# Zeros' term beside the last third of the quantized product, and the next pair's bias pass behind the first convolution's differences

## The chip, the cores and the metric

The kernel runs on one core of a Trainium2 chip. The metric is the device time of one execution in microseconds. The engines that matter here are TensorE (PE in the profile), VectorE (DVE), ScalarE (ACT), GpSimd (POOL), and SyncE (SP), which only issues transfers here. Each engine works through its own queue in order. Engines wait for one another by semaphores.

## What is computed

The input x holds 32 samples of 64 channels by 1024. Two layers follow one another, each with a conditioned chain of four small convolutions (same, upsample with blur, same, blur with downsample) and a product behind it, added to x:

```
x = x + L0_ffn(L0_cond(x, cond))     # gated low-rank experts
x = x + L1_ffn(L1_cond(x, cond))     # product with an int4 weight
# L1_ffn:
W[i, o] = scales[o] * q[i, o] - zeros[o]        # q: 4-bit whole numbers
out = einsum('bsi,io->bso', t, W) + bias
```

For the last line this means that an output is `scales * (t @ q) - zeros * rowsum(t) + bias`, and the residual x is added. `zeros * rowsum(t)` is the zeros' term of the title.

## The kernel before, in words

Two samples share the 128 partitions, so there are 16 pairs per layer. The change lies in the last stage, the second layer's loop over `k` from 16 to 31 (line 1290). In round k the product of pair p = k - 16 runs (`layer1`), and woven into it are the later half of the convolutions of the next pair (`later`, that is `rest`, once for each half h of the pair), the first convolution of the pair after that (`conv`, that is `first`, also once for each half) and the composition of its weights (`weights` and `compose`). `layer1` is a generator: it yields between pieces, and the loop at line 1296 puts the other work between the yields.

**The product.** The 1024 columns plus two (one column of ones, so that column 0 of the product is the row sum) are cut into three thirds c = 0, 1, 2 of 342 columns. For each third PE adds up sixteen matmuls into a PSUM bank (line 1039), eight with the high part of the input tokens and eight with the low part. Then:
- at c = 0, line 1054 takes the negated row sum `nrs` from column 0, and line 1055, one DVE operation over 128x1024, adds `zeros * nrs` to the whole output tile `o`;
- at every c, line 1057 (DVE) multiplies the bank by the scales into `s`, and line 1058 (POOL) adds `s` to its third of `o`;
- after c = 2, line 1060 (SP) sends `o` out.

**The bias pass.** `with_bias(p + 1)` (line 1018; its operation is line 1022, POOL, 128x1024) makes the next pair's `o` from its residual `xb` and the bias. `load_x1` (line 1015, SP) brings `xb`. Both tiles, and all `o` tiles, rotate through three buffers of one tag, so a bias pass can begin only when an older `o` has been sent out.

**The convolutions.** `first` makes `yt` on ACT (line 661), two DVE operations from PSUM (line 666), two DVE differences of SBUF operands (line 671), and then two POOL differences of these (line 674). `rest` is a chain on DVE: 717, 723, 746, the predicated copy 747 (it overwrites the outer columns of a PSUM bank with `re` where a mask from `ident` says so), 148, 773. Line 148 also releases ACT's line 774, behind which on ACT's queue stand the weight copies of lines 594 to 597 and the next `yt` of line 661. `composed2` has the POOL sums of lines 599 and 605.

**What sets the order.** The kernel text is an order of emission. A scheduler in the language builds each engine's queue from it when the program is built: it takes an operation that is ready in its own reckoning, the earlier emitted first. So an operation can stand in a queue far from its line. `tc.issue_after(v)` says that what is emitted in its block stands behind `v` on v's engine: an order of issue only, not a wait.

In round p the pieces are emitted in this order: third 0, high; third 0, low with its end; `later` h = 0; third 1, high; `conv` h = 0; third 1, low with its end; `later` h = 1; third 2, high; `weights`; third 2, low with `with_bias(p + 1)` and its end; `conv` h = 1; `compose`; the sending out.

Of the kernel before, what the change touches and what calls it, by code (L numbers as in the profile page):

```python
# [62 lines left out]
def adaln_ffn_kernel(ctx: ExitStack, tc: tile.TileContext, t, out: bass.AP):  # L63
    nc = tc.nc
# [13 lines left out]
    def cpst(name):  # L78
        return cps.tile([P, H], F32, tag="cps", name=name)
# [4 lines left out]
    def fpst(name):  # L84
        return fps.tile([P, H], F32, tag="fps", name=name)
# [35 lines left out]
    def xdv(n):  # L121
        return cv[:, (n % 2) * XD : (n % 2 + 1) * XD]

    def xev(n):

        o = O_XE + (n % 2) * XE
        return cv[:, o : o + XE]
# [25 lines left out]
    done, tbl, outers = {}, {}, {}  # L153
# [497 lines left out]
    def first(i, n, y):  # L651

        a = al0[:, n : n + 1]
        xe = xev(n)
        w = c0 if i == 0 else xdv(n)[:, : 3 * P].rearrange("p (a b) -> p a b", a=3)
        mid = cpst(f"c{i}_{n}_1")[:, :HQ]
        nc.tensor.matmul(mid, w[:, 1], xe[:, :HQ], start=True, stop=True)  # L659
        yt = wk.tile([P, HQ], F32, tag="yt", name=f"yt{i}_{n}", bufs=2)  # L660
        nc.scalar.activation(yt, mid, AF.Identity, bias=be0[:, n : n + 1], scale=a)  # L661
        yb, yo = y[:, :HQ], y[:, YO : YO + HQ + 1]
        for q, w_, d, o in ((0, HQ, yb, 2 * HQ - 1), (2, HQ - 1, yo[:, 1:HQ], HQ)):
            ps = cpst(f"c{i}_{n}_{q}")[:, :w_]
            done["c"] = nc.tensor.matmul(ps, w[:, q], xe[:, o : o + w_], start=True, stop=True)  # L665
            nc.vector.scalar_tensor_tensor(d, ps, a, yt[:, :w_], ALU.mult, ALU.add)  # L666
        nc.vector.memset(yb[:C, 0:1], 0.0)
        nc.vector.memset(yb[C:, HQ - 1 : HQ], 0.0)
        d = y[:, YD:YO].rearrange("p (a b) -> p a b", a=2)
        for k in range(2):  # L670
            nc.vector.tensor_tensor(d[:, k], yo[:, k : k + HQ], yb, ALU.subtract)  # L671
        e = y[:, YE:].rearrange("p (a two b) -> p a two b", a=2, two=2)
        for k in range(2):
            nc.gpsimd.tensor_tensor(  # L674
                e[:, :, k], d[:, :, 2 * k : 2 * k + HQ - 2 : 2], d[:, :, 1 : HQ - 1 : 2], ALU.subtract
            )
        return y
# [113 lines left out]
    def at(k):  # L791

        return k ^ 1
# [218 lines left out]
    def load_x1(p):  # L1012
        if p < NP:
            v = wk.tile([P, L], F32, tag="w4", name=f"xb_{p}", bufs=3)
            nc.sync.dma_start(v, x1d[p].rearrange("p f j -> p (f j)"))
            residual[NP + p] = v

    def with_bias(p, aux):

        if p < NP:  # L1020
            o = residual[p] = wk.tile([P, L], F32, tag="w4", name=f"o1_{p}", bufs=3)
            nc.gpsimd.tensor_tensor(
                o.rearrange("p (j f) -> p j f", f=4),
                residual.pop(NP + p).rearrange("p (f j) -> p j f", f=4),
                aux[:, 2].rearrange("p (j f) -> p j f", f=4),
                ALU.add,
            )

    def layer1(p, wq, aux):


        o = residual.pop(p)
        for c in range(3):
            if c == 1:
                load_x1(p + 1)
            ps = fpst(f"q{p}_{c}")[:, :QC]
            for j, half in enumerate(toks[f"x1_{p}"]):
                for k in range(NC):
                    nc.tensor.matmul(  # L1039
                        ps,  # L1040
                        half[:, k],
                        wq[at(k)][:, c * QC : (c + 1) * QC],
                        start=(k == 0 and j == 0),
                        stop=(k == NC - 1 and j == 1),
                    )
                if j == 0:
                    yield
            if c == 2:
                with_bias(p + 1, aux)
            a = 2 if c == 0 else 0  # L1050
            cs = slice(c * QC + a - 2, (c + 1) * QC - 2)
            if c == 0:
                nrs = tiny.tile([P, 1], F32, tag="nrs", name=f"nrs{p}")
                nc.vector.tensor_scalar_mul(nrs, ps[:, 0:1], -1.0)
                nc.vector.scalar_tensor_tensor(o, aux[:, 1], nrs, o, ALU.mult, ALU.add)  # L1055
            s = wk.tile([P, QC], F32, tag="yt", name=f"sc{p}_{c}", bufs=2)[:, : QC - a]
            nc.vector.tensor_tensor(s, ps[:, a:], aux[:, 0, cs], ALU.mult)  # L1057
            nc.gpsimd.tensor_tensor(o[:, cs], o[:, cs], s, ALU.add)  # L1058
            yield
        nc.sync.dma_start(out[p], o)  # L1060
# [35 lines left out]
    def conv(k, h, y=None):  # L1096
        if k < len(todo):
            i, n = todo[k][0], 2 * todo[k][1] + h
            y = yv(n) if y is None else y
            ys.setdefault(k, []).append(first(i, n, y))  # L1100
            if i == 1:
                load(k + 1, h)
# [187 lines left out]
    for k in range(NP, 2 * NP):  # L1290
        begin(k + 2)
        tables_of(k + 3)
        outer_of(k + 2)
        main = layer1(k - NP, *second)
        next(main)
        for fs in (
            (),
            ((later, k + 1, 0),),
            ((conv, k + 2, 0),),
            ((later, k + 1, 1),),  # L1300
            ((weights, k + 2),),
        ):
            for f, *v in fs:
                f(*v)
            if k == NP + 1:
                next(set_ends, None)
            next(main)
        conv(k + 2, 1)
        compose(k + 3)
        run(main)  # L1310
        if k == NP:
            set_ends = ends(1, LAST, NP, block(7, [P, 3 * AW], F32, "room3"))
        elif k == NP + 1:
            run(set_ends)
# [44 lines left out]
```

## Time and profile before

| what | value |
|---|---|
| three runs | 956.99, 960.23, 962.82 us (median 960.23) |
| profiled execution, its own time | 961.61 us |
| its span, first to last instruction | 959.8 us |
| granted TensorE clock, mean | 0.979 |
| PE, DVE, ACT, POOL busy | 888.5, 727.6, 324.0, 469.2 us |
| last stage: start of the bias pass in rounds 2 and 14 | 707.17 and 936.56 us |
| L747 (DVE, predicated copy), 24 of them from 707 to 937 us | 432 ns the shortest, mean 1055 ns |
| L1055 (DVE, zeros' term), 13 there | mean 1294 ns |
| L1022 (POOL, bias pass), 16 | 2862 / 2900 / 3882 ns, shortest / median / longest |
| L674 (POOL, differences), 50 from 700 to 940 us | median 616 ns |

A busy time is a sum over the whole span. The chain of work that ended last is followed back from the last instruction to whatever released each step. The timeline lists instructions in order of time, a start and a duration in microseconds, and in square brackets how long the engine sat idle before one and who released it. Two instructions merged in one line are marked x2, and their duration is that of both.

### The profile page before, as it was taken

How to read it: one execution, taken by the hardware profiler on the slowest of the kernel's cores; microseconds unless marked ns; L12 is line 12 of the kernel's file. 1: busy time of each engine (PE TensorE's matmuls, PEld its weight loads, DVE VectorE, ACT ScalarE, POOL GpSimd, SP SyncE). 2: the span in 40 equal slices, each digit the busy share in tenths (PEclk: the TensorE clock that was granted, in tenths of full speed). 3: DMA queues.
4: the chain of work that ended last, by engine and by line, in shares of the span. 5: the costliest groups of instructions: out<-in, count | busy, mean ns of one | idle time of the engine just before them, and what ended most of it. 6: DMA issues, size and time to landing. Idle time of an engine off the chain costs nothing.

```text
span 959.8 us, 14770 instructions
## 1 busy us (share of the span) xinstructions
PE 888.5 (93%) x5069; PEld 789.5 (82%) x5069; DVE 727.6 (76%) x1505; ACT 324.0 (34%) x702; POOL 469.2 (49%) x601
## 2 busy tenths in 40 slices
PE   5778879999999999999999999988899999999996
PEld 4656669999999999984778887778899899988986
DVE  6847786888887788658986666478888888888885
ACT  4224442444443333332431221263233323332320
POOL 4454463444545544455652222234756655665563
PEclk9888979999999999999999999999999999999999
DMA  5721121222222321344566765464322332333221
GB/s 126 232 56 50 50 61 59 74 83 83 72 72 81 85 93 67 111 173 139 169 193 203 208 200 181 154 210 143 105 89 91 114 121 89 102 102 121 83 83 45
DMA packets 48443, 109.81 MB, mean 114 GB/s; under 512 B 12580, under 2 KB 20896, under 8 KB 48368
## 3 DMA queue, kind: packets, MB, share of 16 engines
q1 hardware_dynamic: 46208, 103.42, 34.9%
q0 software_dynamic: 1200, 4.46, 1.4%
q10 hardware_dynamic: 960, 0.99, 0.4%
q8 instruction: 40, 0.66, 0.3%
q14 instruction: 35, 0.29, 0.1%
HBM read 70.97 MB, written 37.88 MB: 113 GB/s over the span
## 4 chain that ended last, share of the span: by engine, by line
PE 30%; DVE 14%; issue 4%; ACT 3%; POOL 2%; DMA 2%; ACTq 0%; POOLq 0%; SPq 0%; DVEq 0%
PE o L806 14%; PE q L1039 6%; PE f L579 2%; PE c L665 2%; DVE cv L671 2%; PE r L701 2%; DVE o L1055 1%; DVE cv L666 1%; PE r L732 1%; DVE r L747 1%; DVE rt L723 1%; DVE r L546 1%; DVE x L967 1%; PE ht L922 1%; PE r L709 1%
## 5 line engine op out<-in xcount | busy, mean ns | idle before, releaser
L674 POOL TENSOR_TENSOR cv<-cv 128x256 f32<-128x256 f32 x124 | 82.5, 665 | 127.3 <-DVE su L849 75.9
L774 ACT CAST thx<-h 128x512 fp32r<-128x512 f32 x60 | 37.1, 618 | 154.5 <-DVE h L148 154.4
L671 DVE TENSOR_TENSOR cv<-cv 128x257 f32<-128x257 f32 x124 | 87.2, 736 | 0.6
L666 DVE SCALAR_TENSOR_TENSOR cv<-c,al,yt 128x257 f32<-128x257 f32 x124 | 56.6, 476 | 31.2 <-ACT yt L661 29.8
L701 PE MATMUL r<-cv 128*128 128x128 f32 x496 | 70.6, 285 | 9.2 <-POOL cv L599 7.8
L1039 PE MATMUL q<-wq,thx 128*128 128x342 f32 x384 | 73.8, 334 | 5.6 <-ACT thx L774 5.6
L701 PEld LDWEIGHTS r<-cv 128*128 128x128 f32 x496 | 66.7, 198 | 12.3 <-POOL cv L599 8.4
L661 ACT ACTIVATE yt<-c,be,al 128x257 f32<-128x257 f32 x64 | 36.3, 568 | 110.9 <-PE c L659 104.5
L1039 PE MATMUL q<-wq,tlx 128*128 128x342 f32 x384 | 73.1, 333 | 0.0
L717 DVE TENSOR_TENSOR rt<-r,tbl 128x256 f32<-128x256 f32 x64 | 26.5, 415 | 61.3 <-PE r L709 57.9
L806 PE MATMUL h<-wa,tdx 128*128 128x352 f32 (+1 forms) x336 | 70.5, 348 | 0.0
L579 PE MATMUL f<-gs,iw 128*128 128x128 f32 (+1 forms) x384 | 70.0, 330 | 0.0
L599 POOL TENSOR_TENSOR cv<-cv 128x256 f32<-128x256 f32 x62 | 46.0, 743 | 47.3 <-ACT cv L597 47.3
L579 PEld LDWEIGHTS f<-gs,iw 128*128 128x128 f32 x384 | 63.4, 193 | 6.5 <-ACT room L519 0.3
L1039 PEld LDWEIGHTS q<-wq,thx 128*128 128x128 f32 x384 | 61.2, 191 | 7.6 <-ACT thx L774 7.0
L1058 POOL TENSOR_TENSOR o<-o,sc 128x342 f32<-128x342 f32 (+1 forms) x48 | 48.2, 1005 | 39.0 <-DVE sc L1057 31.4
L732 PE MATMUL r<-cv 128*128 128x128 f32 x496 | 65.8, 275 | 0.0
L806 PE MATMUL h<-wa,thx 128*128 128x352 f32 (+1 forms) x336 | 64.3, 333 | 0.0
L1039 PEld LDWEIGHTS q<-wq,tlx 128*128 128x128 f32 x384 | 62.8, 192 | 0.7
L806 PE MATMUL o<-wb,thh 128*128 128x512 f32 x224 | 61.7, 407 | 1.1 <-ACT wb L352 0.7
L806 PE MATMUL h<-wa,tlx 128*128 128x352 f32 (+1 forms) x336 | 62.4, 327 | 0.0
L786 POOL TENSOR_TENSOR tdx<-thx,tlx 128x1024 fp32r<-128x1024 f32 x14 | 36.1, 2580 | 52.9 <-ACT tlx L778 48.1
(302 smaller groups left out, 2150.3 us busy)
## 6 DMA issues: line engine op xcount, KB each, us to landing
cv<-in_x_dram SPq DMA_DIRECT2D x64, 256.0 KB
cv<-x1e SPq DMA_DIRECT2D x64, 192.5 KB
x1e<-dd SPq DMA_DIRECT2D x16, 514.0 KB
hgd<-hs SPq DMA_DIRECT2D x16, 512.0 KB
hg<-hgd SPq DMA_DIRECT2D x16, 512.0 KB
x1d<-x SPq DMA_DIRECT2D x16, 512.0 KB
xb<-x1d SPq DMA_DIRECT2D x16, 512.0 KB
out_dram<-o SPq DMA_DIRECT2D x16, 512.0 KB
```

What stands on the lines that cost most here:

```text
L579: done["f"] = nc.tensor.matmul(pv[:, n : n + 2 - k], iw[:, e].rearrange("p a b -> p (a b)"), v, start=(m == 0), stop=(m == len(steps) - 1) ...
L599: (nc.vector if once else nc.gpsimd).tensor_tensor(f[:, 4 * P : 6 * P].rearrange("p (a b) -> p a b", b=P), v[:, :, 0], v[:, :, 1], ALU.add,)
L661: nc.scalar.activation(yt, mid, AF.Identity, bias=be0[:, n : n + 1], scale=a)
L666: nc.vector.scalar_tensor_tensor(d, ps, a, yt[:, :w_], ALU.mult, ALU.add)
L671: nc.vector.tensor_tensor(d[:, k], yo[:, k : k + HQ], yb, ALU.subtract)
L674: nc.gpsimd.tensor_tensor(e[:, :, k], d[:, :, 2 * k : 2 * k + HQ - 2 : 2], d[:, :, 1 : HQ - 1 : 2], ALU.subtract)
L701: nc.tensor.matmul(ps[:, j * P : (j + 1) * P], y[:, j + k : j + k + 2 * P - 1 : 2], w(4 + k), start=(k == 0), stop=(k == 1),)
L732: done["r"] = nc.tensor.matmul(ps[:, j * P : (j + 1) * P], y[:, YE + (2 * q + k) * P : YE + (2 * q + k + 1) * P], w(q + 2 * k), start=True ...
L774: nc.scalar.copy(hi, h)
L806: nc.tensor.matmul(banks[l == 2], toks[key][l][:, order(k)], w[:, cols], start=(k == first and l != 1), stop=(k == last and l in (2, min(n ...
L1039: nc.tensor.matmul(ps, half[:, k], wq[at(k)][:, c * QC : (c + 1) * QC], start=(k == 0 and j == 0), stop=(k == NC - 1 and j == 1),)
L1058: nc.gpsimd.tensor_tensor(o[:, cs], o[:, cs], s, ALU.add)
```

## The change

Three edits:
- `first` keeps the second of its POOL differences (line 674) under the name `done["e"]`.
- `with_bias(p + 1)` is emitted after the high half of third 2, before the yield and so before `weights`, and it is tied behind `done["e"]`, the differences of `conv` h = 0 of the same round. Before, it was emitted after the low half of third 2 and tied to nothing.
- The zeros' term (line 1055) is emitted at c = 2, ahead of that third's scaling, instead of at c = 0. `nrs` is still made at c = 0.

```
@@ first
         for k in range(2):
-            nc.gpsimd.tensor_tensor(
+            done["e"] = nc.gpsimd.tensor_tensor(
                 e[:, :, k], d[:, :, 2 * k : 2 * k + HQ - 2 : 2], d[:, :, 1 : HQ - 1 : 2], ALU.subtract
             )
@@ layer1
                 if j == 0:
+                    if c == 2:
+                        with tc.issue_after(done["e"].ins):
+                            with_bias(p + 1, aux)
                     yield
-            if c == 2:
-                with_bias(p + 1, aux)
             a = 2 if c == 0 else 0
             cs = slice(c * QC + a - 2, (c + 1) * QC - 2)
             if c == 0:
                 nrs = tiny.tile([P, 1], F32, tag="nrs", name=f"nrs{p}")
                 nc.vector.tensor_scalar_mul(nrs, ps[:, 0:1], -1.0)
+            if c == 2:
                 nc.vector.scalar_tensor_tensor(o, aux[:, 1], nrs, o, ALU.mult, ALU.add)
```

More of the change, by code (lines that the diff above doesn't have):

```diff
@@ L673, in first @@
         for k in range(2):
-            nc.gpsimd.tensor_tensor(
+            done["e"] = nc.gpsimd.tensor_tensor(
                 e[:, :, k], d[:, :, 2 * k : 2 * k + HQ - 2 : 2], d[:, :, 1 : HQ - 1 : 2], ALU.subtract
@@ L1046, in layer1 @@
                 if j == 0:
+                    if c == 2:
+                        with tc.issue_after(done["e"].ins):
+                            with_bias(p + 1, aux)
                     yield
-            if c == 2:
-                with_bias(p + 1, aux)
             a = 2 if c == 0 else 0
@@ L1054, in layer1 @@
                 nc.vector.tensor_scalar_mul(nrs, ps[:, 0:1], -1.0)
+            if c == 2:
                 nc.vector.scalar_tensor_tensor(o, aux[:, 1], nrs, o, ALU.mult, ALU.add)
```

## The prediction

> **What bounds the kernel now.** I read first the page's busy times, then busy times by stretch for one round of the last stage, then the chain of waits through that round, then the DVE and POOL timelines of it. All edits lie in that stage.
>
> ```profile
> PE 888.5 (93%) x5069; PEld 789.5 (82%) x5069; DVE 727.6 (76%) x1505; ACT 324.0 (34%) x702; POOL 469.2 (49%) x601
> ```
>
> Over the span PE looks like the bound. The busy times of one round (from bias pass to bias pass: length, then PE, weight load, DVE, ACT, POOL) say something else:
>
> ```profile
> 802.95:821.99 19.04, 17.83 (x116) 16.92 (x116) 16.17 (x32) 6.13 (x14) 11.21 (x13) 1.00 0.33 104
> ```
>
> PE lacks 1.2 us of the round. The chain (start, length, what) shows who holds it:
>
> ```profile
> 816.13 0.58 ACT yt L661
> ...
> 816.73 0.88 DVE cv L666 x2
> ...
> 820.52 1.19 DVE o L1055
> 821.71 0.34 DVE rt L717
> ...
> 822.08 0.70 DVE rt L723
> ...
> 822.92 0.67 PE c L665 x2
> ```
>
> PE's L665 waits for DVE's L723 to free a PSUM bank, and L1055 stands in front of that. DVE and POOL in the same round:
>
> ```profile
> 803.84 0.70 DVE L746 TENSOR_TENSOR r<-r,rt 128x512 f32<-128x512 f32 x1
> 804.57 1.57 DVE L747 COPY_PREDICATED r<-ident,re 128x256 f32<-128x256 int32 x1
> ...
> 808.83 1.47 DVE L671 TENSOR_TENSOR cv<-cv 128x257 f32<-128x257 f32 x2
> 810.22 0.41 DVE L717 TENSOR_TENSOR rt<-r,tbl 128x256 f32<-128x256 f32 x1
> ...
> 811.47 0.70 DVE L746 TENSOR_TENSOR r<-r,rt 128x512 f32<-128x512 f32 x1
> 812.20 0.43 DVE L747 COPY_PREDICATED r<-ident,re 128x256 f32<-128x256 int32 x1
> 812.67 0.69 DVE L148 TENSOR_SCALAR h<-r 128x512 int32<-128x512 int32 x1
> ...
> 814.00 0.50 DVE L1057 TENSOR_TENSOR sc<-q,aux 128x342 f32<-128x342 f32 x1
> 816.73 0.88 DVE L666 SCALAR_TENSOR_TENSOR cv<-c,al,yt 128x257 f32<-128x257 f32 x2 [2.23 <-ACT yt L661]
> ```
> ```profile
> 802.95 2.90 POOL L1022 TENSOR_TENSOR o<-xb,aux 128x1024 f32<-128x1024 f32 x1 [1.41 <-DMA out_dram<-o]
> ...
> 810.45 1.31 POOL L674 TENSOR_TENSOR cv<-cv 128x256 f32<-128x256 f32 x2 [0.42 <-DVE cv L671]
> 815.07 0.74 POOL L599 TENSOR_TENSOR cv<-cv 128x256 f32<-128x256 f32 x1 [3.31 <-ACT cv L597]
> ```
>
> DVE is busy without a break but for 2.23 us. That gap starts when L148 of half 1 (ended 813.36) releases ACT's L774. Behind it stand the six weight copies and `yt`, 3.37 us until DVE's L666. So the round is: DVE from L666 to the end of L148 of half 1, plus 3.37 us of ACT. Whatever is added to or taken from DVE in between counts; what falls into the gap is free up to 2.23 us. Note L747: 0.43 us in half 1, 1.57 us in half 0, where it ends 0.29 us after the bias pass on POOL.
>
> **The change, part by part** (per round, rounds 2 to 13: twelve that have all pieces; X is the end of the second L671 of half 0, 810.30 in this round).
>
> *Zeros' term off third 0.* One L1055, 1.19 us of spacing on the chain: -1.19.
>
> *Bias pass off half 0.* The twelve L747 of half 0 last from 1.16 to 2.34 us, sum 20.1, mean 1.68, against 0.43 unhindered: -1.25. The wait for the sent-out tile (1.41 us idle on POOL) goes too, but it was off the chain.
>
> *Bias pass behind the differences.* L674's pair starts 0.15 after X and ends 1.46 after it. With nothing else in the way L1022 follows at X+1.42 and ends at X+4.32. On DVE L717, L723 and L746 follow X as before ([...]L746 took 0.70 beside L1022 too), and L747 of half 1 comes at X+1.90, half a microsecond after POOL has begun. It would end at X+4.61 instead of X+2.33: +2.28, straight into L148. [...] By the rows (0.43 against 1.57, end tied to POOL's) it is held[...]. I take the rows. [...]it swaps a collision of 1.25 us for one of 2.28.
>
> *Where the zeros' term lands.* It is emitted behind `later` of half 1, but a queue is filled by readiness. In the first layer's stage the trace shows what becomes of ready operations while the chain 717, 723, 746 waits for its own results:
>
> ```profile
> 254.70 0.41 DVE L717 TENSOR_TENSOR rt<-r,tbl 128x256 f32<-128x256 f32 x1
> 255.03 0.78 DVE L638 SCALAR_TENSOR_TENSOR cv<-cv,sty 128x257 f32<-128x257 f32 x1
> 255.75 0.67 DVE L723 TENSOR_TENSOR rt<-r,rt 128x512 f32<-128x512 f32 x1
> ```
>
> They are put between its links. In the last stage L666 of half 0 stands between L148 and L773, although emitted behind both; and L1022 ran in front of third 0's add, emitted at third 2. L1055's last input is POOL's add of third 1 (L1058, 808.99 for 1.03 us, so ended at X-0.28). It is thus ready about when L717 is, five links before L148, and I take it to stand there, either side of L717. In half 1 of before no other ready work competes for these places. The cost: L1055 from X-0.08 to X+1.19 [...]now holds POOL off:
>
> ```profile
> 684.81 3.88 POOL L1022 TENSOR_TENSOR o<-xb,aux 128x1024 f32<-128x1024 f32 x1
> ```
>
> (0.98 over its 2.90, beside an L1055 from 684.63 to 685.93). So the first L674 ends at X+1.67, the second at X+2.36, L1022 runs X+2.32 to X+5.22, and L747 (ready at X+3.09) ends at X+5.51 instead of X+2.33: +3.18, in place of the +2.28. Between L717 and L723 it comes to the same within 0.05. From below: were L1055 behind L148, it would fall into the 2.23 us gap and cost only what it delays POOL's L599 and the add of third 2, behind which the second L671 of half 1 then waits: 0 to 0.3. From above: behind L746 or L747 the whole 1.19 comes after the bias pass: +3.47.
>
> *The rest.* The new place of `load_x1` on SP: it waits for the bias pass's buffer and now comes some 8 us later in the round; behind it stand loads used a round later (L632 was issued at 806.3 for use at 820.7), nothing. `done["e"]`: nothing. Rounds 0 and 1: the 3.88 us bias pass of round 1 stood before small POOL steps that PE waited for (L493 at 690.80); it leaves, 2 to 3 us, and comes back later in the round: -1, between -3 and +1. The last round has no bias pass; its L1055 is ready before third 2 is: 0 to +0.3.
>
> Sum per round: -1.19 - 1.25 + 3.18 = +0.74; times twelve +8.9; minus 1: +7.9 us. PE doesn't bind at 19.8 us a round, as it has 17.83 us of work; L665's wait for L723 moves with DVE. Against the profiled execution: 961.6 + 7.9 = 969.5 (span 959.8 to 967.7). That execution lay 1.4 above the median, so for the median 960.2 + 7.9 = 968.
>
> **The rivals.**
> - *Hidden zeros' term.* L1055 stands behind L148. Per round -1.19 - 1.25 + 2.28 + 0.2 = +0.04: 960. For it: 1.19 fits in 2.23, and it is emitted behind L773. Against: it is ready five links earlier.
> - *Last link.* L1055 stands between L746 and L148: -2.44 + 3.47 = +1.03 a round, 972.
> - *The other side: the bias pass misses L747.* If L1022 begins at X+1.90 or later, by half a microsecond, [...]L1022 fits into POOL's idle 3.31 us before L599 or delays only that. With L1055 hidden as well, DVE saves 2.44 a round, and PE's 17.83 stops it at -1.2: twelve times that, minus 1, is 945. Against: the bias pass has nothing to wait for there; its buffer is free from the sending out on (landed at 802.95) and `xb` can be loaded a round ahead.
> - *The change doesn't do what it says*, its place held by the scheduler as before: excluded for the bias pass by the tie.
>
> **How the numbers follow.** Zeros' term near L717: 0.52, 968, from 963 to 972[...]. Last link: 0.12, 972, up to 976. Hidden: 0.22, 960, 956 to 964. Misses: 0.14, 945, from 935 to 955. The range from 955 to 976 leaves out the last case and little else. A measurement of this kernel can tell about 0.5%, 4.8 us, from no change: slower 0.62, same 0.24, faster 0.14.
>
> **What would show it.** L747: half 0 back at 0.43, half 1 at 2.4 or more, ending 0.29 us behind L1022. L1055 on DVE between the L671 of half 0 and L148, with the first L674 stretched to some 1.5 us. A round of about 19.8 us. The forecast is wrong if L1055 shows between L148 and L666, or if L1022 starts behind L747.

## The result, and the profile after

The changed kernel takes 969.80 us (median of five runs, 966.97 to 971.38) against 960.23 (956.99 to 963.34): ratio 1.0090, 95% interval 1.0061 to 1.0119, so 6 to 11 us slower. The profiled execution took 967.91 us with a span of 966.1, 6.3 more than the span before.

So the forecast of 968 was close and its sign right. Its working was right in part only: the operations stand where it had put them, but the trace shows almost the same round length as before, and the loss in other places. First one round of the last stage in the busy times by stretch (length, PE, weight load, DVE, ACT, POOL):

```profile
801.77:820.94 19.17, 17.85 (x118) 16.82 (x117) 16.57 (x31) 6.13 (x15) 11.74 (x13) 1.00 0.33 104
```

19.17 us where the forecast had 19.8. DVE in that round (the zeros' term is now line 1057, the scaling 1059, POOL's add 1060):

```profile
802.81 0.35 DVE L546 SCALAR_TENSOR_TENSOR r<-w3p,al,tbl 128x128 f32<-128x128 f32 x1
803.08 1.30 DVE L671 TENSOR_TENSOR cv<-cv 128x257 f32<-128x257 f32 x2
...
807.01 0.43 DVE L747 COPY_PREDICATED r<-ident,re 128x256 f32<-128x256 int32 x1
...
810.14 1.48 DVE L671 TENSOR_TENSOR cv<-cv 128x257 f32<-128x257 f32 x2
811.54 1.27 DVE L1057 SCALAR_TENSOR_TENSOR o<-aux,nrs,o 128x1024 f32<-128x1024 f32 x1
812.74 0.41 DVE L717 TENSOR_TENSOR rt<-r,tbl 128x256 f32<-128x256 f32 x1
...
814.71 2.40 DVE L747 COPY_PREDICATED r<-ident,re 128x256 f32<-128x256 int32 x1
```

Every place is as forecast: L747 of half 0 takes 0.43 us, that of half 1 2.40, and the zeros' term stands just ahead of L717. POOL beside it:

```profile
801.51 0.79 POOL L1060 TENSOR_TENSOR o<-o,sc 128x342 f32<-128x342 f32 x1
...
811.76 2.22 POOL L674 TENSOR_TENSOR cv<-cv 128x256 f32<-128x256 f32 x2 [0.43 <-DVE cv L671]
813.94 2.88 POOL L1022 TENSOR_TENSOR o<-xb,aux 128x1024 f32<-128x1024 f32 x1
```

The two L674 last 2.22 us beside DVE's zeros' term (811.54, for 1.27) instead of the 1.31 of before, and L1022 ends 0.29 us before L747 does. And ACT:

```profile
813.89 0.38 ACT L594 COPY cv<-f 128x256 f32<-128x256 f32 x1 [4.55 <-PE f L579]
817.88 0.62 ACT L774 CAST thx<-h 128x512 fp32r<-128x512 f32 x1 [3.61 <-DVE h L148]
```

One of the six weight copies (L594) now stands ahead of L774, in idle time; before, all six stood behind it. That was not foreseen, nor that L546 now stands ahead of the second convolution's L671, nor that third 2's add stands ahead of the second pair of weight sums: the scheduler reordered more than what was edited.

A round of before (797.70 to 816.73) and one of after (801.77 to 820.94), cut at the same operations, in us:

| stretch on DVE | before | after | difference | forecast |
|---|---|---|---|---|
| first L666 of half 1 to L717 of half 0 | 4.90 | 3.28 | -1.62 | -1.19 |
| to the end of L747 of half 0 | 3.54 | 2.40 | -1.14 | -1.25 |
| to the end of the second L671 of half 0 | 4.16 | 4.17 | 0 | 0 |
| to the end of L747 of half 1 | 2.33 | 5.50 | +3.17 | +3.18 |
| to the next L666 (ACT's stretch) | 4.10 | 3.83 | -0.27 | 0 |
| sum | 19.03 | 19.17 | +0.14 | +0.74 |

Over rounds 3 to 13 together it is 210.49 against 210.34. The 6.3 us lie outside: the first L666 of half 1 that ends round 2 starts at 725.06 instead of 721.31 (+3.75), and from the one of round 13 to the end it is 30.59 instead of 28.20 (+2.4). The first figure is rough, for the stage before, which the change doesn't touch, ended 3.9 us earlier in this profile (and anywhere from 640.8 to 647.6 us in the profiles of this document). In round 0 POOL, DVE and PE show this (three views, one after the other):

```profile
674.38 2.90 POOL L1022 TENSOR_TENSOR o<-xb,aux 128x1024 f32<-128x1024 f32 x1
677.24 0.91 POOL L1060 TENSOR_TENSOR o<-o,sc 128x342 f32<-128x342 f32 x1
```
```profile
678.19 1.73 DVE L1057 SCALAR_TENSOR_TENSOR o<-aux,nrs,o 128x1024 f32<-128x1024 f32 x1 [3.27 <-POOL o L1060]
679.84 0.68 DVE L723 TENSOR_TENSOR rt<-r,rt 128x512 f32<-128x512 f32 x1
```
```profile
680.66 0.67 PE L665 MATMUL c<-cv 128*128 128x256 f32 x2 [2.26 <-DVE rt L723]
```

The zeros' term has a new input: POOL's add of third 1. In the steady rounds that add is done in time. In round 0 it stands behind the bias pass, DVE's queue stops at the zeros' term for 3.27 us, L723 is queued behind it, and PE waits 2.26 us for L723's bank. In round 1 the zeros' term waits 2.10 us in the same way.

In round 14 it waits too, but only 0.70 us, and not because the add stands behind the bias pass. There the bias pass begins at 939.84, ahead of L747 of half 0 (940.30), which takes 2.73 us. So DVE's scaling L1059 behind it is late, POOL idles 1.18 us for it before its add, and the zeros' term starts at 945.92, when the add has ended:

```profile
944.98 0.91 POOL L1060 TENSOR_TENSOR o<-o,sc 128x342 f32<-128x342 f32 x1 [1.18 <-DVE sc L1059]
```

### The profile page after: what moved, and what is told of

Its sections match the earlier page's. It is cut to its first block, busy times and chain, and to the rows that moved or that the text cites. A ratio compares the mean times of both kernels' runs of the same rounds, so it can differ in the third digit from the quotient of the medians.

```text
span 966.1 us, 14770 instructions
## 1 busy us (share of the span) xinstructions
PE 886.6 (92%) x5069; PEld 788.6 (82%) x5069; DVE 732.9 (76%) x1505; ACT 324.3 (34%) x702; POOL 473.6 (49%) x601
## 4 chain that ended last, share of the span: by engine, by line
DVE 22%; PE 18%; issue 7%; ACT 3%; POOL 3%; DMA 2%; SPq 0%; ACTq 0%; POOLq 0%; DVEq 0%
PE o L806 13%; DVE r L747 4%; DVE cv L671 3%; DVE cv L666 2%; DVE r L746 2%; DVE rt L723 2%; DVE o L1057 2%; PE q L1039 1%; DVE h L148 1%; ACT thx L774 1%; DVE x L967 1%; POOL o L1022 1%; PE ht L922 1%; DVE rt L717 1%; ACT yt L661 1%
## 5 line engine op out<-in xcount | busy, mean ns | idle before, releaser
L674 POOL TENSOR_TENSOR cv<-cv 128x256 f32<-128x256 f32 x124 | 91.5, 738 | 135.5 <-DVE su L849 75.9
L1039 PE MATMUL q<-wq,thx 128*128 128x342 f32 x384 | 73.5, 334 | 20.2 <-ACT thx L774 20.1
L671 DVE TENSOR_TENSOR cv<-cv 128x257 f32<-128x257 f32 x124 | 87.2, 736 | 0.2
L666 DVE SCALAR_TENSOR_TENSOR cv<-c,al,yt 128x257 f32<-128x257 f32 x124 | 56.7, 476 | 31.8 <-ACT yt L661 27.6
L774 ACT CAST thx<-h 128x512 fp32r<-128x512 f32 x60 | 37.0, 617 | 110.8 <-DVE h L148 110.8
L1060 POOL TENSOR_TENSOR o<-o,sc 128x342 f32<-128x342 f32 (+1 forms) x48 | 43.7, 910 | 61.2 <-DVE sc L1059 61.2
L717 DVE TENSOR_TENSOR rt<-r,tbl 128x256 f32<-128x256 f32 x64 | 26.5, 414 | 59.4 <-PE r L709 58.0
L806 PE MATMUL h<-wa,tdx 128*128 128x352 f32 (+1 forms) x336 | 70.5, 348 | 0.0
L599 POOL TENSOR_TENSOR cv<-cv 128x256 f32<-128x256 f32 x62 | 45.5, 735 | 38.4 <-ACT cv L597 38.4
L806 PE MATMUL h<-wa,thx 128*128 128x352 f32 (+1 forms) x336 | 64.3, 333 | 0.0
L806 PE MATMUL h<-wa,tlx 128*128 128x352 f32 (+1 forms) x336 | 62.4, 327 | 0.0
L806 PE MATMUL o<-wb,thh 128*128 128x512 f32 x224 | 61.4, 405 | 1.1 <-ACT wb L352 0.7
```

The lines of the kernel that those rows point to most:

```text
L599: (nc.vector if once else nc.gpsimd).tensor_tensor(f[:, 4 * P : 6 * P].rearrange("p (a b) -> p a b", b=P), v[:, :, 0], v[:, :, 1], ALU.add,)
L674: done["e"] = nc.gpsimd.tensor_tensor(e[:, :, k], d[:, :, 2 * k : 2 * k + HQ - 2 : 2], d[:, :, 1 : HQ - 1 : 2], ALU.subtract)
L774: nc.scalar.copy(hi, h)
L806: nc.tensor.matmul(banks[l == 2], toks[key][l][:, order(k)], w[:, cols], start=(k == first and l != 1), stop=(k == last and l in (2, min(n ...
L1039: nc.tensor.matmul(ps, half[:, k], wq[at(k)][:, c * QC : (c + 1) * QC], start=(k == 0 and j == 0), stop=(k == NC - 1 and j == 1),)
```

## The experiments

The theory after the two traces (A): what operations of DVE and POOL lose beside each other (+3.17 us at L747 of half 1, -1.14 at that of half 0) nearly cancels in a steady round with what the reordering gives (-1.62 and -0.27), and the loss is that new wait in the first and last rounds. The rival (B) is the prediction's own working. Each diff is against the changed kernel, if nothing else is said. The times stand against the kernel before on the same chip, whose medians were 959.6 to 960.4 us.

**Zeros' term alone moved.** The bias pass is back in its old place.

```
-                        with tc.issue_after(done["e"].ins):
-                            with_bias(p + 1, aux)
                     yield
+            if c == 2:
+                with_bias(p + 1, aux)
```

> Zeros' term at third 2, bias pass where it was. Theory A (read from the two traces: in a steady round the collisions nearly cancel, and what was lost lies in the first rounds and in the last two): a round of about 19.0 us. L747 of half 0 is held longer than before, about 2.2 us or more, since the chain comes sooner and the bias pass still waits for the sent-out tile; L747 of half 1 takes 0.43 us; the last two rounds lose about 2.4 us as in the changed kernel. Time 960 to 963. Theory B (the working of the prediction: the collisions make the whole loss, +0.74 a round): without the bias pass near half 1 the zeros' term costs its 1.19 us there in full and gains nothing at half 0, so a round of about 20.1 us and a time near 972.

Measured: 964.49, ratio 1.0037 (1.0019 to 1.0055). Most rounds take 18.72 us, a little under what A expected; L747 of half 0 1.95 to 2.0 in these, of half 1 0.43; from the L666 of round 13 to the end 31.07. B's round of 20.1 is refuted. The time lies above A's 960 to 963: the first and last rounds lose more than A had put down.

**Bias pass alone moved.** The zeros' term is back at third 0.

```
-            if c == 2:
                 nc.vector.scalar_tensor_tensor(o, aux[:, 1], nrs, o, ALU.mult, ALU.add)
```

> Bias pass behind the differences, zeros' term at third 0 as before. Theory A: L747 of half 0 0.43 us, of half 1 about 2.7 us; the reliefs that came with the moved zeros' term (L546 between the other operations, third 2's add ahead of L599, a weight copy ahead of L774) are absent, so a round of about 20.1 us (19.08 - 1.25 + 2.28), twelve times +1.0 and up to 3 us in the first rounds: 972 to 976. Theory B: the same collisions and +1.03 a round, but -1 in the first rounds: 971. Told apart less by the time than by the rounds 0 to 2 in the trace.

Measured: 971.29, ratio 1.0111 (1.0074 to 1.0147). That is B's time, a little under A's 972 to 976. L747 of half 1 2.69 instead of 0.43, rounds of about 20.16: with the zeros' term at third 0 it costs these 2.26 us in full, and the rounds' share alone (221.07 against 210.34 for rounds 3 to 13) is as large as the whole loss. The first rounds lost nothing here: from the last matmul of the stage before (L806) to the end of round 2 it took 74.5 us, 74.1 in the kernel before and 81.8 in the changed one. So the bias pass by itself is not what the first rounds suffer from, and the loss that A had put down for them did not come.

**Middle rounds alone, end rounds alone.**

```
-                    if c == 2:
+                    if c == 2 and (3 <= p <= 13):      # the other kernel: not 3 <= p <= 13
...
+            if c == 2 and not (3 <= p <= 13):
+                with_bias(p + 1, aux)
...
-            if c == 2:
+            if c == (2 if (3 <= p <= 13) else 0):
```

> The change in rounds 3 to 13 alone; rounds 0 to 2, 14 and 15 as before. Theory A (steady rounds nearly unchanged, 19.17 against 19.08 us): within 2 us of the kernel before, 960 to 962. Theory B (+0.74 a round): eleven times 0.74, about 968.

> The change in rounds 0 to 2, 14 and 15 alone; rounds 3 to 13 as before. Theory A (the loss lies here: about 3.5 us in rounds 0 to 2 and 2.4 us in the last two): about 966. Theory B (the first rounds gain 1 us, the last costs 0.3): 959 to 960.

Measured: middle rounds 961.81, ratio 1.0001 (0.9980 to 1.0022), rounds of 19.17 us; end rounds 965.09, ratio 1.0048 (1.0030 to 1.0066). Theory A, not B: eleven of sixteen rounds changed and nothing lost, the five at the ends changed and 3 to 6 us lost. But A's 2.4 us in the last two rounds are not there: from the L666 of round 13 to the end this kernel takes 28.45 us, 28.20 before and 30.59 in the changed one. The zeros' term of round 14 waits here as well (1.47 us), but L747 of half 0 starts at 936.48, 0.11 us ahead of the bias pass, and takes 0.43 instead of 1.93. A caution: the middle-rounds kernel has the code of before in rounds 0 to 2, yet in its profile they took 77.6 us from the last L806 instead of 74.1. A single trace can't price the first rounds; the timed runs can.

**Zeros' term at third 0 in the end rounds, bias pass moved everywhere.**

```
-            if c == 2:
+            if c == (2 if 3 <= p <= 13 else 0):
                 nc.vector.scalar_tensor_tensor(o, aux[:, 1], nrs, o, ALU.mult, ALU.add)
```

> The change, but in rounds 0 to 2, 14 and 15 the zeros' term stays at third 0; the bias pass is moved in all rounds. Theory A (the loss at the ends is the zeros' term's wait for POOL's add of third 1, which stands behind the bias pass there, and L723 and PE wait behind it): the loss of about 5 us goes, 960 to 962. Rival (the bias pass's new place causes it): 964 to 967.

Measured: 960.24, ratio 0.9992 (0.9970 to 1.0014). The loss is gone, with the bias pass moved in all rounds. It hangs on the place of the zeros' term in rounds 0 to 2, 14 and 15; the bias pass's new place alone doesn't bring it.

**The weight copy behind L774 again.**

```
+            with tc.issue_after(done["th"].ins) if i == 1 and p > 3 else nullcontext():   # th: L774
                 nc.scalar.copy(f8[:, 0::2], pv[:, :, h])
```

> The change with the first weight copy on ACT (L594) tied behind L774, where it stood before; the rest as changed. Theory A: the copy, 0.37 us with its spacing, is back in the stretch from L148 to L666 (3.83 us from the end of L747 in the changed kernel, 4.10 before): +0.27 a round, 19.44 us, about 3 us in all, 972 to 974. Rival (the round is set elsewhere and the copy's place is worth nothing): 969 to 970.

ACT's timeline (its lines are one further down here):

```profile
819.55 0.62 ACT L775 CAST thx<-h 128x512 fp32r<-128x512 f32 x1 [8.53 <-DVE h L148]
820.08 0.37 ACT L595 COPY cv<-f 128x256 f32<-128x256 f32 x1
```

Measured: 972.18, ratio 1.0105 (1.0059 to 1.0151), rounds of 19.43 instead of 19.17. From the end of L747 to the next L666 it is 4.09 again. The -0.27 of the table is this one copy.

**Third 2's add behind the weight sums again.**

```
+            with tc.issue_after(done["sum"].ins) if c == 2 and 2 < p < 14 else nullcontext():
                 nc.gpsimd.tensor_tensor(o[:, cs], o[:, cs], s, ALU.add)
```

> The change with POOL's add of third 2 tied behind the last of the weight sums (L605) in rounds 3 to 13, where it stood before; the rest as changed. Theory A: the add again overlaps the second L671 of half 1[...]: up to +0.43 a round, 19.4 to 19.6 us, 972 to 975. Rival (L546, now between the two, keeps L671 clear of it): +0.1 or less a round, 969 to 971.

Measured: 967.25, ratio 1.0068 (1.0049 to 1.0088), rounds of 19.23. The rival holds: the add's place is worth 0.06 us a round. The time lies under both forecasts, and under the 969.80 of the changed kernel; in part this is round 14 again, where L747 of half 0 now starts 0.10 us ahead of the bias pass and takes 0.43, so that the end from the L666 of round 13 takes 29.66 instead of 30.59.

What is left of the -0.43 in the table's first row lies in L546. In the kernel before both L546 stand behind the second convolution's L671, and the second of them starts beside the first L674 (shortest, median and longest in ns):

```profile
L546 DVE SCALAR_TENSOR_TENSOR r<-w3p,al,tbl x2: 339/528/718, 800.0 to 800.3; 128x128 f32<-128x128 f32 x2
```

It takes 0.72 us and ends 0.15 us behind that L674. In the changed kernel one L546 stands ahead of L671, the other starts ahead of L674, and they take 0.35 and 0.34: the second 0.38 less than before. The six kernels of this document that queue both behind L671 in the steady rounds have 0.72 for the second in each of nine such rounds; in the steady rounds of the changed kernel none is over 0.35. No kernel moved L546 by itself.

**Zeros' term hidden.** It is tied behind L773 of half 1, into DVE's wait for `yt`.

```
-        nc.vector.tensor_tensor(lo, shape(ps), h, ALU.subtract)
+        done["tl"] = nc.vector.tensor_tensor(lo, shape(ps), h, ALU.subtract)
...
             if c == 2:
-                nc.vector.scalar_tensor_tensor(o, aux[:, 1], nrs, o, ALU.mult, ALU.add)
+                with tc.issue_after(done["tl"].ins):
+                    nc.vector.scalar_tensor_tensor(o, aux[:, 1], nrs, o, ALU.mult, ALU.add)
```

> The change with the zeros' term tied behind L773 of half 1, so that it falls into DVE's wait for yt. Theory A: no DVE operation stands between the second L671 and L717 of half 1, so L747 of half 1 waits about 2.7 us from the start of L1022 half a microsecond earlier; but the reorderings that came with the earlier place (L546 between, third 2's add ahead of L599, weight copy ahead of L774) go as well. Round about 19.1 to 19.2 us. In rounds 0 to 2 and 14 L723 no longer waits behind the zeros' term for POOL's add of third 1, so the loss at the ends goes: 959 to 962. Rival: the loss at the ends comes from the bias pass's new place, not from the zeros' term's wait: then 964 to 966 with the same round.

DVE's timeline:

```profile
809.67 2.70 DVE L747 COPY_PREDICATED r<-ident,re 128x256 f32<-128x256 int32 x1
...
813.74 1.27 DVE L1058 SCALAR_TENSOR_TENSOR o<-aux,nrs,o 128x1024 f32<-128x1024 f32 x1
...
816.46 0.88 DVE L666 SCALAR_TENSOR_TENSOR cv<-c,al,yt 128x257 f32<-128x257 f32 x2 [1.03 <-ACT yt L661]
```

Measured: 954.65, ratio 0.9920 (0.9889 to 0.9950). The round is 19.03, a little under the expected 19.1: the idle time before L666 shrank to 1.03 with the zeros' term in it. The loss at the ends is gone and more: from the L666 of round 13 to the end it takes 24.18, not 28.20. That gain I had not expected. In round 14 L747 of half 0 starts 0.11 us ahead of the bias pass and takes 0.43 (1.93 before), and no zeros' term stands in front of L717, so the last product's first matmul starts 10.88 us after that L666 instead of 13.58. PE has been idle for 0.86 us before it instead of 3.55, and its first two groups of eight matmuls take 1.53 and 1.42 us instead of 2.07 and 2.45.

**Bias pass in two operations.**

```
-            nc.gpsimd.tensor_tensor(
-                o.rearrange("p (j f) -> p j f", f=4),
...
+            for u in range(2):
+                js = slice(u * P, (u + 1) * P)
+                nc.gpsimd.tensor_tensor(
+                    o.rearrange("p (j f) -> p j f", f=4)[:, js],
...
```

> The change with the bias pass in two operations of 512 elements. Theory A[...]: L747 of half 1 waits only for the first of the two, about 1.0 us instead of 2.41, and slips in before the second; round from 19.17 to about 17.9 us, where PE with its 17.8 us of work becomes the bound; ends as in the changed kernel: 954 to 957. Rival[...]: L747 waits for both, 2.5 us, round 19.3, 970 or more.

POOL's first half, and DVE:

```profile
809.12 1.55 POOL L1025 TENSOR_TENSOR o<-xb,aux 128x512 f32<-128x512 f32 x1
```
```profile
809.90 1.07 DVE L747 COPY_PREDICATED r<-ident,re 128x256 f32<-128x256 int32 x1
```

Measured: 952.93, ratio 0.9929 (0.9902 to 0.9957), a little under the 954 expected; rounds of 17.97. L747 ends at 810.97, 0.30 us behind the first half (810.67), while the second half ran until 812.35 (1.72 us, where the first took 1.55). Its end goes with that of the first of the two operations.

**No reads on POOL.** The bias pass is replaced by memsets of the same tile.

```
-            nc.gpsimd.tensor_tensor(
...
+            residual.pop(NP + p)
+            for _ in range(3):
+                nc.gpsimd.memset(o, 0.0)
```

> The change with the bias pass replaced by three memsets of the same tile on POOL, which read nothing; the residual and the bias of the second layer are left out of the output. Theory A[...]: L747 of half 1 takes 0.43 us although POOL is as good as busy beside it; round about 17.9 us, PE's; 954 to 957. Rival (L747 waits for any POOL operation, or for something else): it still lasts as long as POOL's memsets do, over 1 us.

POOL, then DVE:

```profile
796.03 2.98 POOL L1024 MEMSET o<- 128x1024 f32 x3
```
```profile
796.82 0.43 DVE L747 COPY_PREDICATED r<-ident,re 128x256 f32<-128x256 int32 x1
```

Measured: rounds of 17.60 and 938.82 us, ratio 0.9758 (0.9717 to 0.9798), lower than the 954 expected. The time also lacks the waits for the residual's transfer at the ends, so only the rows count. The one above would not be enough: the first of the three memsets ended at 796.98, and a copy that ends about 0.3 us behind a POOL operation, as beside the bias pass (0.29) and its first half (0.30), would have ended where L747 did (797.25). Round 0 of the same trace decides it (a count of three, their shortest, median and longest in ns, first and last start; then DVE):

```profile
L1024 POOL MEMSET o<- x3: 951/952/954, 670.6 to 672.6; 128x1024 f32 x3
```
```profile
672.60 0.43 DVE L747 COPY_PREDICATED r<-ident,re 128x256 f32<-128x256 int32 x1
```

L747 begins with the third memset (672.59 to 673.55) and is done in 0.43 us, long before it ends: beside this POOL operation, which reads nothing, it takes the 0.43 us that it takes with POOL idle. So it doesn't wait for just any POOL operation. That the reads of the bias pass are what it waits for was the author's theory; the run fits it but doesn't show it alone, as a memset differs from the bias pass in more than its reads.

**Both improvements**, and both with the bias pass at its old place:

> Both: zeros' term behind L773 and bias pass in two operations. Theory A: L747 of half 1 about 1.3 us; DVE chain some 17.7 us, PE's work 17.8, so a round of about 17.9 us, and the loss at the ends gone: 944 to 949. Rival (PE or the weight copies on ACT bind already above 18.5): 953 to 956.

> Kernel before with the zeros' term behind L773 of half 1 and the bias pass in two operations, but at its old place behind the sent-out tile. Theory A: L747 of half 0 waits for the first half alone, to about 1.4 us; DVE chain 7.05 + 4.17 + 2.33 + 0.72 + 3.37 = 17.6 us a round, as with the new place: 936 to 941, so that moving the bias pass is worth nothing by itself. Rival (at the old place the wait for the sent-out tile binds): L747 of half 0 over 1.8 us, round 18.2 or more, 945 to 950.

Measured: 938.13, ratio 0.9739 (0.9698 to 0.9780) with the new place; 942.39, ratio 0.9789 (0.9750 to 0.9827) with the old. One round of the first:

```profile
807.41:825.05 17.64, 17.64 (x118) 17.06 (x117) 15.98 (x32) 6.03 (x14) 11.41 (x13) 1.00 0.36 113
```

PE has no idle time in the 17.64 us: it is the bound now. Its busy time is not a fixed sum, though: the same 118 matmuls come to 17.85 us in the round of the changed kernel, and the whole round is 17.97 us in the kernel with two halves alone and 17.60 in the one without reads. This version beats both kernels, by 22 us (medians) the one before. At the old place, where 936 to 941 was expected, the rounds are 17.70 to 18.08; the intervals of the two overlap, so the move of the bias pass is worth 0.2 us a round by the traces and not clearly anything by the times. The gain lies in the two small edits. With the new place I had expected 944 to 949; the end from the L666 of round 13 takes 24.29 us here, the same unforeseen gain as above.

## Why the prediction was right, and where it wasn't

*What bounds the kernel.* Right: the round is DVE from L666 to L148 of half 1 plus ACT's stretch, with PE close behind. The last version, with PE busy for 17.64 us of 17.64, stops at PE's work.

*Zeros' term off third 0, -1.19.* Too small: -1.62 in the row that contains it. The term missed 0.43: 0.06 is the add's place by its own run, and 0.38 is the second L546, which took 0.72 us beside POOL's L674 before and 0.34, beginning ahead of L674, after.

*Bias pass off half 0, -1.25.* Right (-1.14 in this round).

*Bias pass behind the differences, with the zeros' term in front of L717, +3.18.* Right to 0.01, and each link of it: the two L674 took 2.22 us beside the zeros' term, L1022 began 2.32 us behind the second L671 for that, and L747 took 2.40 us and ended 0.29 behind L1022. The rows of before (0.43 against 1.57) were rightly believed.

*"The rest": "Rounds 0 and 1 ... -1, between -3 and +1", and round 14, for which there is no term.* This step failed. It looked at where the bias pass leaves, and said of the zeros' term's new input only that it is ready "about when L717 is", which is true of a steady round alone. In rounds 0 and 1 the add of third 1 stands behind the bias pass on POOL; DVE waits for it, 3.27 and 2.10 us, with its chain behind, and PE waits for DVE. In round 14 L747 takes 2.73 us beside the bias pass, and the add is late for it. The end rounds cost 1.0048 when changed alone. The last round's own term, "0 to +0.3", was right: from PE's last matmul to the end it is 5.45 us instead of 5.25.

*The missing term.* Nothing was put down for the order of the untouched operations. With the zeros' term moved, L594 slipped ahead of L774: -0.27 a round, shown by its own run.

So the sum was right by luck, from two wrong terms: +8.9 us forecast for twelve rounds against next to nothing measured (0.15 us over rounds 3 to 13), and -1 at the ends forecast against +4.6 by the end rounds' own timing (+6.1 between the two profiles). The two parts changed alone give 1.0001 and 1.0048, the whole 1.0090 (1.0061 to 1.0119). The rest, some 0.4%, is about as large as the intervals; the whole change with one add put back gave 1.0068. About 2 us of it can be read from the traces: when the steady rounds are changed too, the bias pass of round 14 comes ahead of L747 (the end takes 30.59 instead of 28.45). Whether there is more in the rest than spread stays open.

*The rivals.* The hidden zeros' term, put at 960 if the scheduler had chosen that place, gives 954.65; its round was right (19.03 against +0.04 on 19.08), its last rounds were not. The other side, the bias pass missing L747, was put at 945 with PE as the bound; the halves reach that bound in another way, 17.64 us a round.

## What to carry to other kernels

When an operation is moved past another engine's work, ask at every stretch of the program, the first and last rounds too, whether what it newly waits for is done by then; in round 0 the zeros' term waited 3.27 us on DVE, L723 stood behind it, and PE waited 2.26 us for L723. Where a short operation on the critical chain takes longer beside a long one of another engine, try the long one in pieces: with the bias pass in two halves L747 of half 1 took 1.07 us instead of 2.40, and the round 17.97 instead of 19.17. Look also at which of the two starts first: in round 14 L747 took 2.73 us where the bias pass began 0.46 us ahead of it, and 0.43 with the end rounds alone changed, where it began 0.11 us ahead of the bias pass. And after an edit compare the whole order of each queue: untouched operations may stand elsewhere, and be worth as much as the edit.

## What the runs showed of the hardware

- L747, the predicated copy on DVE, took 0.43 us with POOL idle (812.20 in the kernel before, 807.01 in the changed one). Where the bias pass on POOL had begun before it, it took 2.40 us (changed kernel, the round from 801.77), 2.70 (zeros' term hidden) and 2.73 (changed kernel, round 14), and ended 0.29 or 0.30 us behind the bias pass. Where it began 0.10 or 0.11 us ahead of the bias pass (round 14 of three kernels), it took 0.43; within a POOL memset of 0.95 us, too.
- With the bias pass in two halves, L747 took 1.07 us and ended 0.30 us behind the first half, 1.38 before the second ended.
- The second L546 on DVE took 0.72 us where it ended 0.15 us behind a POOL L674 that ran beside it (kernel before), and at most 0.35 in the steady rounds of the changed kernel.
- Two L674 on POOL took 1.31 us together in the round of before, and 2.22 beside one DVE operation of 1.27 in that of after.

Why they take longer beside each other is not shown by these runs; the times are.
